# A convolution stage spread over two places, channel statistics moved to ScalarE, and two POOL products merged

## The chip, the cores and the metric

One NeuronCore of one Trainium2 chip runs the kernel. The metric is device time in microseconds, from the first to the last instruction and what lies around it; a lower time is better. Engine names follow the profile: PE is TensorE (matrix products), PEld its weight loads, DVE is VectorE, ACT is ScalarE, POOL is GpSimd and SP is SyncE, which here only starts DMAs.

## The reference

The input `x` is 32 x 96 x 56 x 56 in fp32. Two layers follow each other. The first is a ConvNeXt block; the second passes the image as a sequence of 3136 tokens through two Mamba blocks and ends with a batch normalisation over all images and tokens. Cut to what matters:

```
# layer 0
h = conv7x7_depthwise(x) + conv_b
h = gelu(layernorm_c(h) @ w1 + b1) @ w2 + b2
x = transpose(h) * layer_scale + x
# layer 1
seq = tokens(x)                                     # 32 x 3136 x 96
for i in range(2):
    h = layernorm(seq[i]);  xs, z = split(h @ in_w)
    xc = silu(causal_conv4(xs));  dt, Bm, Cm = split(xc @ xproj_w)
    delta = softplus(dt @ dt_w + dt_b)
    h_t = exp(delta * A) * h_(t-1) + delta * Bm * xc    # 192 channels x 16 states
    y = (sum_s h * Cm + Dp * xc) * silu(z);  seq = seq + y @ out_w
out = fus_w @ concat(seq, relu(mean(x) @ gp_w)) + fus_b
out = (out - mean_bhw(out)) * rsqrt(var_bhw(out) + eps) * bn_g + bn_b + x
```

The last line needs the mean and the variance of `out` per channel over 32 x 3136 values: these are the statistics that the change moves.

## The kernel before, in words

An image is cut in four chunks of 784 tokens (`CH`), a chunk in two halves of 392 (`HC`). A *stage* is one chunk of one image in one of the two Mamba layers, so there are 32 x 4 x 2 = 256 stages. The order alternates: from stage 2 on, even stages are layer `i == 1` and odd stages are layer `i == 0` of the next chunk.

A stage has 24 *steps* (`NSTEP`): six groups `j` of 32 channels times four groups `g` of four states. Step `n` is `scan(n)`: on DVE a product `w` (L847) of the spread `u` in PSUM with the row `B`, then the recurrence (L854, TENSOR_TENSOR_SCAN) that writes one of four slots of the ring `h`; then POOL multiplies the slot with `C` (L858), and three steps later (`LAG`) `add_up` sums it on PE into `y` (L891). ACT computes the factor `exp(delta*A)` (L805) one or two steps ahead. For `j` in `POOLED` (2 and 5, steps 8 to 11 and 20 to 23) the product `w` is made by POOL instead (L831), so there DVE has only scans to do.  `spread` (L820) is a selection product on PE that brings `u` into PSUM for four steps; it is issued at the end of steps 3, 7, 11, 15 and 23, where DVE's product of the following step needs it.

All other work of the kernel is cut into pieces and laid into the steps by hand. A piece is a pair of a slot number and a function; slot 12.4 means "after the scan of step 12, ordered by 0.4 among the pieces there", a negative slot belongs to the stage before, one of 24 and more to the stage after, and a piece marked `True` runs on DVE ahead of the scan of its step. Every engine's queue keeps this order (`manual_schedule`). The pieces are:

- `prep` of the next stage: layer norm of `seq` (centre, square, mean, root at slots 11 to 13, `norm` on DVE within step 15), projections, `softplus` (writes `dl` at step 4), the products `u = dl * xc` on POOL (L655), and the DMAs that lay `u` out for the pooled groups (`uu`, `us`) and `delta` for the exps (`d4`, three buffers).
- `post` of the stage before: `project` (7.5), `move` from PSUM into `seq` on ACT (L750, slots 9 and 10) and, when the stage before was layer 1, `stat` (L757): two bn_stats on DVE (L760) within step 13, a DMA of their 12 numbers per channel into `stats_d`, and the DMA of `seq` into `o_d`. This falls into odd stages.
- `block0`: half a chunk of layer 0 in each of stages 2 to 249: centre, square, mean and root (L371, L372) at slots 11.3 to 12.8, `norm` on DVE (L419, writes `hz`) ahead of scan 14, then `up` (L424), gelu, `down` (L443) and the residual on ACT (L450) at 18.3.
- `conv`: the depthwise convolution for images 11 to 31. The first 11 images are convolved before the stages begin. For the rest there are three groups of seven images, 48 pairs of channels each, so 144 pieces of work, one in each of stages 2 to 145. Two channels of 56 rows lie on 112 partitions; a vertical band matrix (`band`, 112 x 7 x 112) holds the taps, and seven products (L503), one per horizontal tap, sum 7 images x 56 columns = 392 columns in PSUM. `load` brings `band` and `xpad` (one buffer each) at slot -10, the taps run at 7.7 to 10.4, and `store` at 11.05 adds the bias on ACT (L512) and sends the result to `conv_d` (L515).

PSUM tile `ps2`, which the taps write, has one buffer that the layer-0 block, the projections and the taps use in turn. The tag `sq` has three buffers for squares and the convolution's output. `seq` has four.

After the stages, bn_aggr (L967) makes the mean and the variance of the stored statistics, and a last loop reads `o_d` and `x1_d` and writes the output.

Of the kernel before, what the change touches and what calls it, by code (L numbers as in the profile page):

```python
# [34 lines left out]
F32 = mybir.dt.float32  # L35
I32 = mybir.dt.int32
AF = mybir.ActivationFunctionType
ALU = mybir.AluOpType
AX = mybir.AxisListType
# [4 lines left out]
L = H * W  # L44
C = 96
# [6 lines left out]
NCH = 4  # L52
CH = L // NCH
HC = CH // 2
# [7 lines left out]
def convnext_mamba_kernel(  # L62
# [31 lines left out]
    nc = tc.nc  # L94
    B = x.shape[0]

    dram = ctx.enter_context(tc.tile_pool(name="dram", bufs=1, space=DRAM))
# [3 lines left out]
    NB = 7  # L101
    b0 = B - 3 * NB if B > 3 * NB else B
    groups = [(0, b0)] + [(b, b + NB) for b in range(b0, B, NB)]
    conv_d = [
        dram.tile([C * H, (hi - lo) * W], F32, name=f"conv_d{lo}", tag=f"conv_d{lo}")
        for lo, hi in groups
    ]
    band_d = dram.tile([C // 2, 2 * H, 7 * 2 * H], F32, name="band_d")
    stats_d = dram.tile([C, B * NCH, 12], F32, name="stats_d")
    x1_d = [dram.tile([C, L], F32, name=f"x1_d{b}", tag=f"x1_d{b}") for b in range(B)]  # L110
    o_d = [dram.tile([C, L], F32, name=f"o_d{b}", tag=f"o_d{b}") for b in range(B)]

# [82 lines left out]
    for i in range(2):  # L195
# [12 lines left out]
        if i == 1:  # L208

            d["res"] = fw1  # L210
            for q in range(NQ):
                ps = sups.tile([128, 512], F32, name="ps", tag="nps")
# [5 lines left out]
                ps = sups.tile([128, 512], F32, name="ps", tag="nps")  # L218
# [29 lines left out]
    for k in range(2):  # L248
        t = const.tile([C + 1, 3 + CH], F32, name=f"hn{k}", tag=f"hn{k}")
        nc.vector.memset(t[C : C + 1, :], 1.0)  # L250
        hns.append(t)
        t = const.tile([C + 1, HC], F32, name=f"hz{k}", tag=f"hz{k}")
# [4 lines left out]
    R2 = 2 * H  # L257
    GB = (b0 + 1) // 2
    cb = const.tile([R2, C // 2], F32, name="cb")
# [69 lines left out]
    with ExitStack() as main:  # L329
# [13 lines left out]
        def tok(a):  # L343
            return slice(a * HC, (a + 1) * HC)
# [138 lines left out]
        xpad = wp.tile([R2, NB, W + 6], F32, name="xpad", tag="xpad", bufs=1)  # L483
        nc.vector.memset(xpad, 0.0)

        def conv(g, p):
            lo, hi = groups[g]
            v = {}

            def load():  # L490
                v["band"] = wp.tile([R2, 7, R2], F32, name="band", tag="band", bufs=1)
                nc.sync.dma_start(v["band"].rearrange("p k n -> p (k n)"), band_d[p])
                nc.sync.dma_start(
                    xpad[:, :, 3 : 3 + W],
                    x[lo:hi, 2 * p : 2 * p + 2, :].rearrange("b c (h w) -> (c h) b w", w=W),
                )

            def taps_(dws):
                def piece():
                    if dws[0] == 0:  # L500
                        v["ps"] = psum(2)
                    for dw in dws:
                        nc.tensor.matmul(  # L503
                            v["ps"][0:R2, 0 : NB * W], v["band"][:, dw, :],
                            xpad[:, :, dw : dw + W], start=(dw == 0), stop=(dw == 6),
                        )

                return piece

            def store():  # L510
                t = wp.tile([R2, HC], F32, name="sq", tag="sq", bufs=3)
                nc.scalar.activation(  # L512
                    t[:, 0 : NB * W], v["ps"][0:R2, 0 : NB * W], AF.Identity, bias=cb[:, p : p + 1]
                )
                nc.sync.dma_start(conv_d[g][p * R2 : (p + 1) * R2, :], t[:, 0 : NB * W])  # L515

            return [
                (-10, load), (7.7, taps_((0,))), (8.2, taps_((1,))), (8.6, taps_((2,))),
                (9.2, taps_((3,))), (9.6, taps_((4,))), (10.2, taps_((5,))), (10.4, taps_((6,))),
                (11.05, store),  # L520
            ]


# [6 lines left out]
        def prep(S):  # L530
# [117 lines left out]
                    nc.sync.dma_start(ddv[a], dl[rows(a)])  # L648
                S.d4 = []

            def product(q):
                def piece():
                    if q == 0:
                        S.u = wp.tile([128, NQ, HC], F32, name="u", tag="u", bufs=1)
                    nc.gpsimd.tensor_tensor(S.u[:, q], v["dl"][:, q], S.xc[:, q], ALU.mult)  # L655

                return piece

            def store_u(k):
                def piece():  # L660
                    j = POOLED[k]
                    if k == 0:
                        v["uu"] = bcd.tile([len(POOLED), 32, CH], F32, name="uu", tag="uu")
                        S.us = {}
                    for a in range(2):
                        r = 64 * a + 32 * (j % 2)
                        nc.sync.dma_start(v["uu"][k, :, tok(a)], S.u[r : r + 32, j // 2, :])

                return piece
# [34 lines left out]
            elif S is stages[3]:  # L704
# [13 lines left out]
                (t[6] + 0.2, silu("z", None)), (t[7], dbl), (t[8], dbl_out),  # L718
                (max(10.2, t[8] + 1.2), load_bc((0, 1))), (max(13.2, t[8] + 2.2), load_bc((2, 3))),
                (t[9], dt), (t[10], softplus),  # L720
                (max(16.2, t[10] + 1), product(0)), (max(17.2, t[10] + 2), product(1)),
                (max(18.3, t[10] + 3.1), store_u(0)), (25.2, product(2)), (26.3, store_u(1)),
                (max(17, t[10] + 2), load_d4(0)), (max(18, t[10] + 3), load_d4(1)),
                (max(20, t[10] + 3.2), load_u(0)), (23, load_d4(2)),
                (26, load_d4(3)), (32.9, load_u(1)), (30, load_d4(4)), (35, load_d4(5)),
# [2 lines left out]
        def post(S):  # L728


            i, b, c = S.i, S.b, S.c
            v = {}

            def project():
                v["ps"] = [psum(0), psum(1)]
                for a in range(2):
                    nc.tensor.matmul(
                        v["ps"][a][0:C, 0:HC], S.d["res"], S.seq[:, tok(a)],
                        start=True, stop=False,
                    )  # L740
                for q in range(NQ):
                    for a in range(2):
                        nc.tensor.matmul(
                            v["ps"][a][0:C, 0:HC], S.d["ow"][rows(a), q, :], S.z[rows(a), q, :],
                            start=False, stop=(q == NQ - 1),
                        )

            def move(a):
                def piece():
                    nc.scalar.activation(  # L750
                        S.seq[:, tok(a)], v["ps"][a][0:C, 0:HC], AF.Identity,
                        bias=batch_bias[b] if i == 1 else 0.0,
                    )

                return piece

            def stat():  # L757
                st = wp.tile([C, 2, 6], F32, name="stat", tag="stat", bufs=2)
                for a in range(2):
                    nc.vector.bn_stats(st[:, a, :], S.seq[:, tok(a)])  # L760
                nc.sync.dma_start(stats_d[:, b * NCH + c, :], st.rearrange("p a k -> p (a k)"))
                nc.sync.dma_start(o_d[b][:, c * CH : (c + 1) * CH], S.seq)
                del seqs[b, c]

            pieces = [(7.5, project), (9, move(0)), (10, move(1))]
            if i == 1:
                pieces.append((13, True, stat))
            return pieces


# [190 lines left out]


    mv = const.tile([C, 2], F32, name="mv")
    with tc.tile_pool(name="sp", bufs=1) as sp:
        stats = sp.tile([C, B * NCH * 2, 6], F32, name="stats")
        nc.sync.dma_start(stats.rearrange("p (n a) k -> p n (a k)", a=2), stats_d)
        nc.vector.bn_aggr(mv, stats)  # L967
    sc = const.tile([C, 1], F32, name="sc")
    nc.scalar.activation(sc, mv[:, 1:2], AF.Sqrt, bias=eps_c[0:C])
    nc.vector.reciprocal(sc, sc)  # L970
# [74 lines left out]
```

## Time and profile before

| what | value |
| --- | --- |
| median of 3 runs | 17518.44 us (17515.35 to 17520.57) |
| the profiled execution's own time | 17504.21 us |
| its span, first to last instruction | 17502.5 us |
| mean granted PE clock | 0.936 |
| busy: DVE, POOL, PE, ACT | 16171.5, 15632.4, 15285.5, 11224.1 us |
| first scan starts / last scan starts | 641.8 us / 17126.4 us |
| DMA moved | 2346.89 MB, 134 GB/s |

A group of instructions in the profile is a line, an engine, an operation, the tile written and the tiles read, their shapes, how many there are, then the busy time with the mean of one in ns, and the idle time of the engine just ahead of them with what ended most of it. PE's products are pipelined: a fp32 product leaves two records, one per pass, and records overlap, so what a product costs is read from the distance of starts. In a list of waits a row is: engine and line that waited, what ended the wait, total us, times, longest. In the timeline a row is start, duration, engine, line and operation, and in brackets the idle time ahead of it.

### The profile page before, as it was taken

What the parts mean: (1) busy time and instruction counts of PE and PEld (TensorE: products, weight loads), DVE (VectorE), ACT (ScalarE), POOL (GpSimd) and SP (SyncE); (2) the same over time, 40 slices, a digit from 0 to 9 for tenths busy, and PEclk for the clock granted to TensorE, in tenths of its full rate; (3) what the DMA queues carried; (4) which work ended last, traced back from release to release, by engine and by line L of the source; (5) the groups of instructions that cost most, each with busy time, mean ns of one, the idle gap of its engine ahead of it and who ended that gap; (6) DMA issues with size and microseconds to landing.
All of it is one profiled execution on the core that took longest, in us unless ns stands there. A gap on an engine that the chain in (4) does not pass through costs nothing. (4 is left out here: it accounts for less than half of the span.)

```text
span 17502.5 us, 212206 instructions
## 1 busy us (share of the span) xinstructions
PE 15285.5 (87%) x65976; PEld 5191.4 (30%) x65976; DVE 16171.5 (92%) x12592; ACT 11224.1 (64%) x17479; POOL 15632.4 (89%) x8993
## 2 busy tenths in 40 slices
PE   7799999999999999999999988888888888888880
PEld 5233333333333333333333322222222222222220
DVE  7499999999999999999999999999999999999994
ACT  1566666666666666666666666666666666666653
POOL 0499999999999999999999999999999999999991
PEclk9799999999999999999999999999999999999985
DMA  4355555555555555555555555555555555555548
GB/s 102 87 139 138 138 135 136 140 139 139 138 135 138 137 140 138 134 137 137 139 139 134 136 126 128 128 125 125 126 129 127 125 126 126 129 127 124 126 116 273
DMA packets 1403525, 2346.89 MB, mean 134 GB/s; under 512 B 627654, under 2 KB 775154, under 8 KB 1402388
## 3 DMA queue, kind: packets, MB, share of 16 engines
q1 hardware_dynamic: 1395220, 2294.77, 53.1%
q10 hardware_dynamic: 7168, 38.54, 0.6%
q8 instruction: 520, 8.52, 0.2%
q14 instruction: 617, 5.05, 0.1%
HBM read 1929.50 MB, written 402.80 MB: 133 GB/s over the span
## 5 line engine op out<-in xcount | busy, mean ns | idle before, releaser
L858 POOL TENSOR_TENSOR da<-h,bc 128x784 f32<-128x784 f32 x6144 | 11295.8, 1863 | 884.9 <-DVE h L854 721.8
L854 DVE TENSOR_TENSOR_SCAN h<-da,st,w 128x784 f32<-128x784 f32 x3072 | 5662.4, 1843 | 314.3 <-ACT st L865 8.6
L891 PE MATMUL y<-da,ssum 128*32 128x392 f32 x24576 | 5086.0, 533 | 562.9 <-POOL da L858 561.2
L847 DVE TENSOR_TENSOR w<-w,bc 128x784 f32<-128x784 f32 x4096 | 3996.0, 976 | 311.0 <-PE w L820 139.5
L831 POOL TENSOR_TENSOR da<-us,bc 128x784 f32<-128x784 f32 x2048 | 3818.4, 1864 | 2.3 <-DMA us<-uu 2.3
L805 ACT ACTIVATE da<-d,A 128x784 f32<-128x784 f32 x4096 | 3753.9, 941 | 44.8 <-DMA d<-dd 28.6
L805 ACT ACTIVATE w<-d,A 128x784 f32<-128x784 f32 x2048 | 1879.6, 918 | 2659.7 <-DVE h L854 2403.2
L854 DVE TENSOR_TENSOR_SCAN h<-w,st,da 128x784 f32<-128x784 f32 x1536 | 2712.5, 1827 | 5.7 <-ACT st L865 4.6
L891 PEld LDWEIGHTS y<-da,ssum 128*32 128x32 f32 x24576 | 1097.3, 114 | 4106.8 <-issue 2359.5
L576 PE MATMUL ps<-hn,wx 97*64 97x392 f32 x12288 | 2260.4, 502 | 7.4 <-DVE hn L564 7.4
L854 DVE TENSOR_TENSOR_SCAN h<-da,w 128x784 f32<-128x784 f32 x1024 | 1826.4, 1784 | 106.7 <-ACT st L865 4.0
L820 PE MATMUL w<-u,sel 64*128 64x392 f32 x4096 | 1032.9, 583 | 719.0 <-DVE h L854 719.0
L655 POOL TENSOR_TENSOR u<-dl,xc 128x392 f32<-128x392 f32 x768 | 791.6, 1031 | 561.3 <-ACT dl L641 561.3
L576 PEld LDWEIGHTS ps<-hn,wx 97*64 97x64 f32 x12288 | 792.0, 136 | 1420.6 <-issue 1098.9
L885 PE MATMUL y<-xc,D 128*128 128x392 f32 x1536 | 796.8, 605 | 306.9 <-DVE z L872 305.2
L351 ACT ACT_TABLE_LOAD x759 | 973.8, 1283 | 14.7 <-PEq L1032 0.8
L854 DVE TENSOR_TENSOR_SCAN h<-w,da 128x784 f32<-128x784 f32 x512 | 872.2, 1766 | 0.0
L360 ACT ACTIVATE sq<-ps 96x392 f32<-96x392 f32 x768 | 340.6, 490 | 827.2 <-PE ps L355 529.7
L503 PE MATMUL ps<-xpad,band 112*112 112x392 f32 x2016 | 816.1, 520 | 0.0
L633 PE MATMUL ps<-dbl,dtw 6*64 6x392 f32 x3072 | 684.2, 509 | 100.3 <-ACT dbl L611 100.3
L820 PEld LDWEIGHTS w<-u,sel 64*128 64x128 f32 x4096 | 327.2, 196 | 1424.7 <-DVE h L854 1262.4
L865 ACT COPY st<-h 128x2 f32<-128x2 f32 x2304 | 417.5, 181 | 426.3 <-DVE h L854 424.9
(112 smaller groups left out, 14111.0 us busy)
## 6 DMA issues: line engine op xcount, KB each, us to landing
bc<-bd SPq DMA_DIRECT2D x4096, 196.0 KB, 5.2
d<-dd SPq DMA_DIRECT2D x6144, 98.0 KB, 2.6
us<-uu SPq DMA_DIRECT2D x2048, 98.0 KB, 2.2
dd<-dl SPq DMA_DIRECT2D x512, 294.0 KB, 3.8
uu<-u SPq DMA_DIRECT2D x1024, 49.0 KB, 1.6
band<-band_d SPq DMA_DIRECT2D x144, 343.0 KB, 7.4
cv<-conv_d SPq DMA_DIRECT2D x256, 147.0 KB, 2.4
xin<-in_x SPq DMA_DIRECT2D x128, 294.0 KB, 3.0
```

The costliest lines, as they stand in the source:

```text
L351: nc.scalar.preload_act_table_set("natural_log_exp_and_others")
L503: nc.tensor.matmul(v["ps"][0:R2, 0 : NB * W], v["band"][:, dw, :], xpad[:, :, dw : dw + W], start=(dw == 0), stop=(dw == 6),)
L576: nc.tensor.matmul(v["x", q][rows(a), 0:HC], weights[:, k, 64 * q : 64 * q + 64], v["hn"][:, o : o + HC], start=(k == 0), stop=(k == last),)
L655: nc.gpsimd.tensor_tensor(S.u[:, q], v["dl"][:, q], S.xc[:, q], ALU.mult)
L805: nc.scalar.activation(e, S.d4[j], AF.Exp, scale=S.d["A"][:, j, g : g + 1])
L820: nc.tensor.matmul(S.u4[:, 512 * a : 512 * a + HC], sel[rows(a), j % 2, :], S.u[rows(a), j // 2, :], start=True, stop=True,)
L831: nc.gpsimd.tensor_tensor(t, S.us[j], S.bcs[g][:, 0, :], ALU.mult)
L847: nc.vector.tensor_tensor(halves(db), S.u4.rearrange("p (a b) -> p a b", a=2)[:, :, 0:HC], halves(S.bcs[g][:, 0, :]), ALU.mult,)
L854: nc.vector.tensor_tensor_scan(ring[:, g, :], S.e.pop((j, g)), db, 0.0 if c == 0 else d["st"][:, j, g : g + 1], ALU.mult, ALU.add,)
L858: nc.gpsimd.tensor_tensor(da, ring[:, g, :], S.bcs[g][:, 1, :], ALU.mult)
L885: nc.tensor.matmul(S.y[:, 0:HC], S.d["D"][:, q, :], S.xc[:, q, :], start=True, stop=False)
L891: nc.tensor.matmul(S.y[r0 : r0 + 32, 0:HC], ssum, da[:, tok(a)], start=False, stop=(g == NG - 1),)
```

## The change

The convolution of a stage is cut in two parts by images: part 0 has the first four of the seven (224 columns), part 1 the last three (168 columns). Part 0's taps stay at slots 7.7 to 10.4 and its store at 11.05; part 1's taps go to slots 18.5 to 22.2 and its store to 22.9. The loads of `band` and `xpad` move from slot -10 to slot -1. The statistics leave DVE: `move` in layer 1 also accumulates the sum per channel (`accum_out`), and at slots 17.2 and 18.2 ACT squares the deviations from the half's own mean and accumulates them; four numbers per channel go to `stats_d` instead of twelve, and the sums are combined at the end by ten DVE operations in place of bn_aggr. The save of `seq` into `o_d` becomes a piece of its own at 12.9. The first two of the three POOL products `u` become one of 784 columns at slot 16.9.

```diff
-            def taps_(dws):
+            def tap(part, dw):
+                first, last = PARTS[part]
                 def piece():
...
+                    nc.tensor.matmul(
+                        v["ps"][0:R2, 0 : (last - first) * W], v["band"][:, dw, :],
+                        xpad[:, first:last, dw : dw + W], start=(dw == 0), stop=(dw == 6),
+                    )
...
-            def store():
-                t = wp.tile([R2, HC], F32, name="sq", tag="sq", bufs=3)
-                nc.scalar.activation(
-                    t[:, 0 : NB * W], v["ps"][0:R2, 0 : NB * W], AF.Identity, bias=cb[:, p : p + 1]
-                )
-                nc.sync.dma_start(conv_d[g][p * R2 : (p + 1) * R2, :], t[:, 0 : NB * W])
+            def store(part):
+                first, last = PARTS[part]
+                n = (last - first) * W
+                def piece():
+                    t = wp.tile([R2, HC], F32, name="sq", tag="sq", bufs=3)
+                    nc.scalar.activation(
+                        t[:, 0:n], v["ps"][0:R2, 0:n], AF.Identity, bias=cb[:, p : p + 1]
+                    )
+                    nc.sync.dma_start(
+                        conv_d[g][p * R2 : (p + 1) * R2, first * W : last * W], t[:, 0:n]
+                    )
...
+            at = (7.7, 8.2, 8.6, 9.2, 9.6, 10.2, 10.4), (18.5, 18.6, 19.2, 20.2, 21.2, 21.3, 22.2)
             return [
-                (-10, load), (7.7, taps_((0,))), (8.2, taps_((1,))), (8.6, taps_((2,))),
-                (9.2, taps_((3,))), (9.6, taps_((4,))), (10.2, taps_((5,))), (10.4, taps_((6,))),
-                (11.05, store),
+                (-1, load), (11.05, store(0)), (22.9, store(1)),
+                *[(at[part][dw], tap(part, dw)) for part in range(2) for dw in range(7)],
             ]
...
-                    nc.gpsimd.tensor_tensor(S.u[:, q], v["dl"][:, q], S.xc[:, q], ALU.mult)
+                    nc.gpsimd.tensor_tensor(
+                        S.u[:, lo:hi], v["dl"][:, lo:hi], S.xc[:, lo:hi], ALU.mult
+                    )
...
-                (max(16.2, t[10] + 1), product(0)), (max(17.2, t[10] + 2), product(1)),
-                (max(18.3, t[10] + 3.1), store_u(0)), (25.2, product(2)), (26.3, store_u(1)),
+                (max(16.9, t[10] + 1.5), product(0, 2)), (max(18.3, t[10] + 3.1), store_u(0)),
+                (25.2, product(2, 3)), (26.3, store_u(1)),
...
+                    nc.scalar.activation(
+                        S.seq[:, tok(a)], v["ps"][a][0:C, 0:HC], AF.Identity, bias=batch_bias[b],
+                        accum_out=v["st"][:, a : a + 1],
+                    )
...
-            def stat():
-                st = wp.tile([C, 2, 6], F32, name="stat", tag="stat", bufs=2)
-                for a in range(2):
-                    nc.vector.bn_stats(st[:, a, :], S.seq[:, tok(a)])
-                nc.sync.dma_start(stats_d[:, b * NCH + c, :], st.rearrange("p a k -> p (a k)"))
+            def stat(a):
+                def piece():
+                    neg = wp.tile([C, 1], F32, name="neg", tag="neg", bufs=2)
+                    nc.scalar.activation(neg, v["st"][:, a : a + 1], AF.Copy, scale=-1.0 / HC)
+                    t = wp.tile([R2, HC], F32, name="sq", tag="sq", bufs=3)[0:C]
+                    nc.scalar.activation(
+                        t, S.seq[:, tok(a)], AF.Square, bias=neg,
+                        accum_out=v["st"][:, 2 + a : 3 + a],
+                    )
+                    if a == 1:
+                        nc.sync.dma_start(stats_d[:, b * NCH + c, :], v["st"])
...
+            def save():
                 nc.sync.dma_start(o_d[b][:, c * CH : (c + 1) * CH], S.seq)
...
-                pieces.append((13, True, stat))
+                pieces += [(12.9, save), (17.2, stat(0)), (18.2, stat(1))]
...
-        nc.vector.bn_aggr(mv, stats)
+        nc.vector.tensor_reduce(part, st[:, :, 0:2], AX.X, ALU.add)
+        nc.vector.tensor_reduce(mean, part, AX.X, ALU.add)
+        nc.vector.tensor_scalar(mean, mean, 1.0 / (B * L), None, ALU.mult)
+        nc.vector.tensor_scalar(dev, st[:, :, 0:2], 1.0 / HC, mean, ALU.mult, ALU.subtract)
+        nc.vector.tensor_tensor(dev, dev, dev, ALU.mult)
+        nc.vector.tensor_scalar(dev, dev, float(HC), None, ALU.mult)
+        nc.vector.tensor_tensor(dev, dev, st[:, :, 2:4], ALU.add)
+        nc.vector.tensor_reduce(part, dev, AX.X, ALU.add)
+        nc.vector.tensor_reduce(var, part, AX.X, ALU.add)
+        nc.vector.tensor_scalar(var, var, 1.0 / (B * L), None, ALU.mult)
```

## The prediction on record

> **What bounds the kernel now.** I read the page's busy table and costliest groups first, then the waits of VectorE, then single stages in the timeline. The 256 stages run from 642 to 17130 us, so a stage is about 64.3 us; everything that pays must pay there, per stage.
>
> ```profile
> PE 15285.5 (87%) x65976; PEld 5191.4 (30%) x65976; DVE 16171.5 (92%) x12592; ACT 11224.1 (64%) x17479; POOL 15632.4 (89%) x8993
> ...
> L854 DVE TENSOR_TENSOR_SCAN h<-da,st,w 128x784 f32<-128x784 f32 x3072 | 5662.4, 1843 | 314.3 <-ACT st L865 8.6
> ...
> L655 POOL TENSOR_TENSOR u<-dl,xc 128x392 f32<-128x392 f32 x768 | 791.6, 1031 | 561.3 <-ACT dl L641 561.3
> ...
> L503 PE MATMUL ps<-xpad,band 112*112 112x392 f32 x2016 | 816.1, 520 | 0.0
> ```
>
> DVE and POOL are both nearly full. Which of them leads is told by who waits: POOL waits for DVE's scan (L858 <- DVE h, 721.8 us in all), while DVE never waits noticeably for POOL. Measured from the scans' ends, POOL's product of step 12, 14 and 16 starts 0.1 us after its scan (POOL is waiting there, 2.9 to 3.5 us a stage) and lags by at most 2.3 us elsewhere, less than the four scans that the ring `h` allows. So DVE sets the stage, and a microsecond of POOL alone is worth nothing. The waits of DVE, in the stages with a convolution (2 to 145) and then in those without, are:
>
> ```profile
> DVE w L847 <- PE w L820: 127.0, 116, 4.8
> ```
>
> ```profile
> DVE hz L419 <- ACT ps L372: 73.8, 69, 2.3
> DVE w L847 <- PE w L820: 12.5, 6, 4.8
> ```
>
> The reader is to see two different stalls. With a convolution DVE waits for PE's spread of `u` (L820) ahead of step 12; without one it waits for the normalisation of `block0` (L419). Averaged from the starts of the scans, step 11 takes 3.97 us with a convolution and 3.28 without; step 13 takes 3.2 and 4.2 (even stages). Stage 46 shows the first, on DVE and PE:
>
> ```profile
> 3635.99 7.05 DVE L854 TENSOR_TENSOR_SCAN h<-w,st,da 128x784 f32<-128x784 f32 x4
> 3644.83 0.98 DVE L847 TENSOR_TENSOR w<-w,bc 128x784 f32<-128x784 f32 x1 [1.79 <-PE w L820]
> ```
>
> ```profile
> 3641.56 0.85 PE L891 MATMUL y<-da,ssum 128*32 128x392 f32 x4
> 3642.34 1.58 PE L503 MATMUL ps<-xpad,band 112*112 112x392 f32 x4
> 3643.85 0.93 PE L820 MATMUL w<-u,sel 64*128 64x392 f32 x4
> ```
>
> PE has no idle time from step 4 to 13 there; the last taps stand straight ahead of the spread. The cause of the backlog is a half-speed clock around steps 4 to 6:
>
> ```profile
> 3625.40:3634.20 8.80, 8.80 (x31) 2.61 (x30) 8.36 (x7) 5.18 (x8) 8.67 (x6) 0.63 0.44 115
> ```
>
> PE, by contrast, has room in steps 19 to 23 (stage 61):
>
> ```profile
> 4634.69 0.93 PE L885 MATMUL y<-xc,D 128*128 128x392 f32 x2 [1.18 <-DVE z L872]
> 4635.54 2.17 PE L891 MATMUL y<-da,ssum 128*32 128x392 f32 x12
> 4638.32 0.85 PE L891 MATMUL y<-da,ssum 128*32 128x392 f32 x4 [0.61 <-POOL da L858]
> 4639.93 0.93 PE L820 MATMUL w<-u,sel 64*128 64x392 f32 x4 [0.75 <-DVE h L854]
> ```
>
> [...] without a convolution PE is idle 3.7 us in steps 7 to 11, and the centring products then take 0.86 us a record instead of 0.49 (granted clock 0.61 from 13538 to 13550). [...] Here Square without one is 490 ns (L360), Identity with one 571 (L750). [...]
>
> **The change part by part.**
>
> *Convolution.* A tap is two passes, 0.33 us apart in the timeline, so 0.66 us; seven are 4.6. Steps 7 to 10 keep 4/7 of the columns, so PE gains 3/7 of 4.6 = 2.0 us ahead of the spread. The excess of step 11 over 3.29 us sums to 103 us over 144 stages (the 127.0 above less the usual 0.17 us gap of 116 waits and less a start-up wait of 4.8 agrees). Clipping each stage's excess by 2.0 leaves 11 us: gain 92. What is late next is `hz` at step 13: ScalarE's exponential for it ends 0.5 to 0.9 us before DVE arrives (even stages), 1.2 to 1.7 (odd). It moves with PE, so no new wait in even stages.
> Part 1 costs PE 7 x 2 passes x 168/392 x 0.33 = 2.0 us, plus about 0.1 us start for each of five isolated groups (first record 0.59 against 0.49): 2.5 us. No row shows 168 columns; if its weight load (L503's LDWEIGHTS, 174 ns a pass, hidden now behind 0.33) bounds a pass instead of the 0.14 that I take, it is 14 x 0.174 + 0.5 = 2.9; nothing can make it less than 2.0. The idle time shown above is 1.18 + 0.61 + 0.75 = 2.5. The spread of the next step 0 then starts about when it does now; it ends 0.9 us before DVE needs it (4640.8 against 4641.7), which is the cover. Behind part 1's store on ACT stand the exps of steps 25 on, needed over 3 us later. The store itself is one more ACTIVATE: 83.2 us/144 = 0.58 becomes about 0.44 + 0.39, in ACT idle time.
> On SP, the loads of `band` and `xpad` move from step 14 to 23, behind three d4 loads, cv, x1, uu, us and the new store. They wait for the last tap, at about step 22.5; behind them stand d4(3), needed at step 10, and the second uu store, needed at 9. They land in 7.4 and 8.0 us and have 20 us. Cost nothing; were SP held 15 us longer, d4(3) would reach ACT late.
>
> *Statistics.* bn_stats leaves DVE: step 12 is 3.69 us in odd stages and 2.98 in even ones, 0.71 each. In 72 odd stages with a convolution: 51 us. In the 55 without, DVE would only wait for `hz` instead: odd stages take 64.35 us, even ones 64.28, so 0.07 x 55 = 4. ACT gets, in each odd stage, two accumulator reads of 0.19 (L450's row) at steps 9 and 10, and at 17 and 18 two times 0.2 (a small copy, L865: 181 ns) + 0.58 + 0.19 = 1.9 us. ACT is idle there for 3.47 us, waiting for L443 (stage 61); behind them stand the residual (L450), which waits for PE anyhow, and the exps of step 20. On SP the statistics' store moves from 13 to 18 and waits for ACT ahead of x1 and uu, which wait later still. Uncovered it would be 2.3 us x 128 = 295. The 0.4 at steps 9 and 10 delays the third Square at most; I charge 4 us for odd stages whose `hz` slack goes. At the end bn_aggr (7.08 us) becomes ten small operations, about 3.3, and the last stage's statistics cost 0.9 more: gain 3.
>
> *Product.* One of 784 columns costs 1.86 (L858's row) against 2 x 1.03: POOL saves 0.2 x 256 = 51 us, worth 0 since POOL waits for DVE. The product of step 17 comes 0.8 us later, used three steps later.
>
> *Sum:* 92 + 51 + 4 + 3 - 4 = 146 us. From the profiled 17504.2 (span 17502.5) that is 17358; the median of the runs shown is 14.2 higher, so 17372.
>
> **Rivals.** (A) *Only the statistics pay*: after a half-clock spell PE stays late, or `hz` takes over the stall. Then 51 + 4 + 3 = 58: 17460. For it: `hz` is 0.5 us from being late. Against: it is fed by the same PE queue that gets earlier.
> (B) *PE goes cold* in steps 8 to 11, since they are thinned out, and conv stages become as those without: even 63.96 to 64.28, odd 64.61 to 64.28, which cancels; 7 remain: 17511. Against: steps 20 to 22 are idle 2.5 us of 5.2 now and keep the clock; 8 to 10 would be about a quarter idle.
> (C) *Slower: a half clock in steps 18 to 23*, now filled to the brim. A spell of 6.8 us [...] loses 3.4 us of PE work; less the cover of 0.9 it holds the next stage's first DVE product by 2.5. In two thirds of the stages (as often as at steps 4 to 6): 96 x 2.5 = 240, less 146: 17612. It decides from 1.9 us lost in every stage. Against: no half clock shows there today, with less work.
> (D) That the change does not do what it says: the order of instructions has bn_stats gone, and seven taps of 224 and seven of 168 columns at the places named.
>
> **How the numbers follow.** Forecast 0.78 (own range 100 to 180 us of gain: 17338 to 17418), A 0.10, B 0.08, C 0.04. The range takes in the forecast and A: 17338 to 17465. A measurement tells about 0.2%, 35 us, from no change: faster 0.88, same 0.08, slower 0.04.
>
> **What would show it.** Right: step 11 near 3.3 us in conv stages, the L847 <- L820 wait under 40 us, odd and even conv stages both near 63.3 us, stages without unchanged near 64.3, POOL's idle time down by about 1 us a stage with nothing lost. Wrong: new DVE waits for ACT at steps 17 to 19 or for the spread at step 23, or clock below 1 in steps 8 to 11.

## The result, and the profile after

| what | before | after |
| --- | --- | --- |
| median of 5 runs each, us | 17518.44 (17514.75 to 17522.98) | 17438.04 (17421.82 to 17446.45) |
| the profiled execution: own time, span, us | 17504.21, 17502.5 | 17446.45, 17444.6 |
| mean granted PE clock | 0.936 | 0.929 |

The change makes the kernel 80 us faster: ratio 0.9953, 95% interval 0.9938 to 0.9967. 146 us were forecast. The median lies above the forecast's own range (17338 to 17418) and inside the wider one, up to 17465, that takes in rival A. The runs of after spread over 25 us and the profiled one is the slowest of them, so the profiled pair differs by less, 57.9 us of span; the ledger below adds up to that.

The page after has the same groups under new line numbers: the scan is L885 (was L854), DVE's product L878 (L847), POOL's product L889 (L858), the spread L851 (L820), the sum into `y` L922 (L891), `z` L903 (L872), the taps L506 (L503), POOL's `u` L666 (L655). First the busy table and the groups:

```profile
PE 15502.9 (89%) x67992; PEld 5472.5 (31%) x67992; DVE 16064.8 (92%) x12345; ACT 11460.0 (66%) x18647; POOL 15605.6 (89%) x8737
...
L666 POOL TENSOR_TENSOR u<-dl,xc 128x784 f32<-128x784 f32 (+1 forms) x512 | 737.5, 1440 | 564.1 <-ACT dl L652 564.1
L506 PE MATMUL ps<-xpad,band 112*112 112x224 f32 (+1 forms) x4032 | 1003.0, 358 | 0.0
```

The parts of the edit that concern DVE and POOL did to those engines what they say: DVE has 106.7 us less to do, POOL's `u` costs 54 us less (POOL's busy time as a whole 27), and PE is busy for 217 us more. Now the waits of DVE in the stages with a convolution (a row is who waited for what, total us, times, longest), then those in the stages without:

```profile
DVE w L878 <- PE w L851: 122.0, 158, 4.8
DVE z L903 <- PE y L922: 21.8, 19, 1.2
```

```profile
DVE hz L419 <- ACT ps L372: 95.5, 73, 2.3
```

The row that the change should have emptied, DVE's product waiting for the spread, was 127.0 us with 116 waits and is 122.0 with 158. The row alone would say that nothing was gained. It mixes two places, though: the same line waits ahead of step 12 and ahead of step 0. Only the steps, taken apart by the starts of the scans, tell them apart. Sums are over the 144 stages with a convolution:

| where | before | after | difference, us | forecast |
| --- | --- | --- | --- | --- |
| step 11, excess over 3.29 us | 102.6 | 28.3 | -74 | -92 |
| step 12, odd stages | 3.69 each | 2.97 each | -51 | -51 |
| step 19, excess over 2.21 | 3.1 | 23.2 | +20 | 0 |
| step 23, excess over 3.02 | -0.5 | 64.6 | +65 | 0 |
| stages without a convolution: even, odd | 64.21, 64.35 each | 64.21, 64.07 each | -15 | -4 + 4 |
| from the last scan's start to the end | 376.1 | 371.2 | -5 | -3 |

The sum is -60; no other step of these 144 stages changes by more than 1.5 us in sum. A stage with a convolution now takes 64.13 us (even; 63.96 before) or 63.88 (odd; 64.61 before); 63.3 was forecast for both. So the stall ahead of step 12 did shrink, but a new one stands ahead of step 0. In stage 60 the trace shows it on PE and on DVE (start, duration, and in brackets the idle time ahead):

```profile
4553.97 0.54 PE L506 MATMUL ps<-xpad,band 112*112 112x168 f32 x2
4554.45 0.85 PE L922 MATMUL y<-da,ssum 128*32 128x392 f32 x4
4555.23 0.83 PE L506 MATMUL ps<-xpad,band 112*112 112x168 f32 x4
4555.99 0.85 PE L922 MATMUL y<-da,ssum 128*32 128x392 f32 x4
4556.77 0.54 PE L506 MATMUL ps<-xpad,band 112*112 112x168 f32 x2
4557.24 0.93 PE L851 MATMUL w<-u,sel 64*128 64x392 f32 x4
```

```profile
4558.22 0.98 DVE L878 TENSOR_TENSOR w<-w,bc 128x784 f32<-128x784 f32 x1 [1.18 <-PE w L851]
```

No row on PE has an idle time any more, where stage 61 before had 1.18, 0.61 and 0.75: PE works without a pause up to the spread, and DVE stands for 1.18 us.

In about a quarter of the stages there is, on top of that, a *spell*: a stretch in which PE is granted half its clock (0.50 in the trace's records of it). Stage 61 after, step 14 and the steps behind it, on PE and as a window (length, busy time of PE, PEld, DVE, ACT, POOL, the granted clock, DMA share, GB/s):

```profile
4598.72 0.93 PE L851 MATMUL w<-u,sel 64*128 64x392 f32 x4 [1.80 <-DVE h L885]
4599.58 0.90 PE L922 MATMUL y<-da,ssum 128*32 128x392 f32 x4
4600.41 4.29 PE L424 MATMUL ps<-hz,w_sb 97*128 97x392 f32 x6
```

```profile
4600.00:4610.00 10.00, 10.00 (x34) 3.40 (x30) 9.43 (x9) 7.61 (x13) 8.90 (x6) 0.66 0.52 116
```

PE waits 1.80 us for a scan, and the six passes of `up` (L424) just behind then take 4.29 us: the granted clock was 0.50 from 4600.26 to 4607.09, and 1.00 in the 12 us before 4600.

Of the 142 stages from 4 to 145, 36 have such a spell in steps 14 to 18 and 106 have none. Without one, the spread of step 0 starts 2.83 us after scan 22 and step 23 takes 3.21 us; with one, it starts at 3.91 and step 23 takes 4.26 and step 19 2.88. Before, 39 stages had a spell there too, and in them the spread started at 1.87 us, just as in the other stages, and step 23 took 3.02. The spells are not new; what is new is that they cost something.

### The profile page after: what moved, and what is told of

It is laid out like the page before. It is cut to its first block, busy times and chain, and to the rows that moved or that the text cites. A ratio compares the mean times of both kernels' runs of the same rounds, so it can differ in the third digit from the quotient of the medians.

```text
span 17444.6 us, 217495 instructions
## 1 busy us (share of the span) xinstructions
PE 15502.9 (89%) x67992; PEld 5472.5 (31%) x67992; DVE 16064.8 (92%) x12345; ACT 11460.0 (66%) x18647; POOL 15605.6 (89%) x8737
## 5 line engine op out<-in xcount | busy, mean ns | idle before, releaser
L889 POOL TENSOR_TENSOR da<-h,bc 128x784 f32<-128x784 f32 x6144 | 11267.2, 1856 | 855.6 <-DVE h L885 734.9
L885 DVE TENSOR_TENSOR_SCAN h<-da,st,w 128x784 f32<-128x784 f32 x3072 | 5664.5, 1844 | 326.4 <-ACT st L896 8.6
L922 PE MATMUL y<-da,ssum 128*32 128x392 f32 x24576 | 5147.1, 542 | 407.2 <-POOL da L889 403.2
L878 DVE TENSOR_TENSOR w<-w,bc 128x784 f32<-128x784 f32 x4096 | 3996.2, 976 | 300.9 <-PE w L851 132.7
L885 DVE TENSOR_TENSOR_SCAN h<-w,st,da 128x784 f32<-128x784 f32 x1536 | 2712.2, 1827 | 5.9 <-ACT w L836 4.8
L922 PEld LDWEIGHTS y<-da,ssum 128*32 128x32 f32 x24576 | 1094.8, 115 | 3681.1 <-issue 2141.1
L885 DVE TENSOR_TENSOR_SCAN h<-da,w 128x784 f32<-128x784 f32 x1024 | 1827.0, 1784 | 109.1 <-ACT st L896 4.3
L851 PE MATMUL w<-u,sel 64*128 64x392 f32 x4096 | 1026.5, 580 | 655.0 <-DVE h L885 654.0
L666 POOL TENSOR_TENSOR u<-dl,xc 128x784 f32<-128x784 f32 (+1 forms) x512 | 737.5, 1440 | 564.1 <-ACT dl L652 564.1
L506 PE MATMUL ps<-xpad,band 112*112 112x224 f32 (+1 forms) x4032 | 1003.0, 358 | 0.0
L885 DVE TENSOR_TENSOR_SCAN h<-w,da 128x784 f32<-128x784 f32 x512 | 872.3, 1766 | 0.0
L506 PEld LDWEIGHTS ps<-xpad,band 112*112 112x112 f32 x4032 | 583.7, 175 | 832.5 <-issue 770.0
L851 PEld LDWEIGHTS w<-u,sel 64*128 64x128 f32 x4096 | 327.9, 196 | 1255.6 <-DVE h L885 1096.3
```

Source lines behind the costliest of these rows:

```text
L506: nc.tensor.matmul(v["ps"][0:R2, 0 : (last - first) * W], v["band"][:, dw, :], xpad[:, first:last, dw : dw + W], start=(dw == 0), stop=(dw ...
L666: nc.gpsimd.tensor_tensor(S.u[:, lo:hi], v["dl"][:, lo:hi], S.xc[:, lo:hi], ALU.mult)
L851: nc.tensor.matmul(S.u4[:, 512 * a : 512 * a + HC], sel[rows(a), j % 2, :], S.u[rows(a), j // 2, :], start=True, stop=True,)
L878: nc.vector.tensor_tensor(halves(db), S.u4.rearrange("p (a b) -> p a b", a=2)[:, :, 0:HC], halves(S.bcs[g][:, 0, :]), ALU.mult,)
L885: nc.vector.tensor_tensor_scan(ring[:, g, :], S.e.pop((j, g)), db, 0.0 if c == 0 else d["st"][:, j, g : g + 1], ALU.mult, ALU.add,)
L889: nc.gpsimd.tensor_tensor(da, ring[:, g, :], S.bcs[g][:, 1, :], ALU.mult)
```

## The experiments

The theory: the two parts that were sized at nothing are the loss. Part 1 of the convolution takes more PE time in steps 18 to 23 than the idle time and the cover there, which costs a little in every stage, and it has used up the idle time in which PE made good a half-clock spell of steps 13 to 17, which costs a lot in a quarter of them. The rivals: the statistics on ACT, or the one long POOL product, hold something up; or the loss is the residual at step 11, which lies behind the pooling pieces of every eighth stage. Times are medians of 4 to 13 runs, and each ratio is taken against runs of before on the same chip. Those runs of before have medians of 17516 to 17521 us on all chips, so kernels of different chips are set side by side below. Excesses and spells are read from one execution of each kernel.

**The statistics alone.** After, with the convolution and the products of before:

```diff
-                (-1, load), (11.05, store(0)), (22.9, store(1)),
+                (-10, load), (7.7, taps_((0,))), ... (10.4, taps_((6,))),
+                (11.05, store),
```

> Only the statistics are changed; the convolution is whole at its old place and the products are two. Theory 1 (the parts add up; the statistics take 0.71 us from step 12 of every odd stage with a convolution and a little of those without): 51 + 15 + 5 = about 70 us less, 17448. Step 11 keeps its mean of about 4.0 us, step 23 its 3.02, DVE's wait for the spread its 127 us. Rival (the two parts need each other, since the time that DVE saves at step 12 is only waited for elsewhere unless PE is relieved too): under 30 us less, 17490 or more, with new waits of hz on ScalarE in the stages with a convolution.

Measured: 17444.1 us, ratio 0.9957 (0.9945 to 0.9970), 77 us below before. Step 12 in odd stages goes from 3.69 to 2.97; steps 19 and 23 have no excess (-0.6 and 1.0 us). Step 11 keeps its whole stall: 118.9 us of excess, and the row of the spread stays full:

```profile
DVE w L865 <- PE w L838: 139.7, 109, 4.0
```

So ACT's part of the change holds nothing up, and the statistics alone are worth nearly all that the whole change is worth.

**The convolution alone.** Before, with only the divided convolution:

```diff
-                (-10, load), (7.7, taps_((0,))), ... (10.4, taps_((6,))),
-                (11.05, store),
+                (-1, load), (11.05, store(0)), (22.9, store(1)),
```

> Only the convolution is cut in two. Theory 1 (the gain at step 11 is given back at steps 19 and 23, where part 1 uses up PE's idle time): about -74 at step 11, +20 at step 19 and +65 at step 23, which is +11: 17530, within 20 us of before. Rival (what is lost at step 23 comes from ScalarE's statistics at steps 17 and 18 or from the merged product, not from part 1): step 23 stays at 3.02 and the time falls by 70 or more, to 17450 or less.

Measured: 17496.6 us, ratio 0.9988 (0.9980 to 0.9996), 24 us below before. It is lower than I expected, since step 11's excess fell to 8.1 us where I had carried over after's 28. The sign of the loss is as the theory has it: step 23 has 73.0 us of excess and step 19 10.0, with bn_stats still on DVE. The row has more waits than that of before, and is shorter in sum:

```profile
DVE w L858 <- PE w L831: 108.8, 165, 4.8
```

94 us come in at step 11 and 80 go out at steps 19 and 23. The stall is paid again twelve steps later.

**The product alone.** Before, with only the merged POOL product:

```diff
-                    nc.gpsimd.tensor_tensor(S.u[:, q], v["dl"][:, q], S.xc[:, q], ALU.mult)
+                    nc.gpsimd.tensor_tensor(
+                        S.u[:, lo:hi], v["dl"][:, lo:hi], S.xc[:, lo:hi], ALU.mult
+                    )
```

> Only the two first POOL products are merged. Theory 1 (POOL waits for DVE, so its work is worth nothing): POOL busy 50 us less, time within 10 us of before, 17508 to 17528. Rival (POOL sets part of the stage): 30 to 50 us less, 17470 to 17490.

Measured: 17509.75 us, ratio 0.9995 (0.9987 to 1.0003). POOL's busy time falls from 15632.4 to 15599.4 us, and the time is not distinguishable from before: POOL waits for DVE, so what it saves it waits.

**Part 1 packed.** After, with its seven taps in two groups that end before step 21, instead of five that reach to step 22:

```diff
-            at = (7.7, 8.2, 8.6, 9.2, 9.6, 10.2, 10.4), (18.5, 18.6, 19.2, 20.2, 21.2, 21.3, 22.2)
+            at = (7.7, 8.2, 8.6, 9.2, 9.6, 10.2, 10.4), (18.5, 18.6, 18.7, 18.8, 20.2, 20.3, 20.4)
```

> The whole change, with part 1's taps as two groups of four and three at 18.5 to 18.8 and 20.2 to 20.4 instead of five groups at 18.5 to 22.2. Theory 1 (part 1's place decides: with it the spread ahead of step 0 starts 2.83 us after scan 22 in undisturbed stages, 0.95 later than before; fewer groups and no tap behind step 20's POOL results bring it back by 0.5 us or more): step 23 falls from 3.47 to about 3.2 us, 30 to 45 us less than the change, 17395 to 17410. Rival (the half-clock spell of steps 14 to 18 alone holds the spread; the order of the taps is indifferent): step 23 stays at 3.4 or more and the time at 17438 within 15.

Measured: 17368.42 us, ratio 0.9916 (0.9903 to 0.9930), 70 us below after, where 30 to 45 were expected. The same products on PE, only in other places, bring the time to what had been forecast for the change. Stage 60 on PE, then the row of waits:

```profile
4524.61 1.40 PE L506 MATMUL ps<-xpad,band 112*112 112x168 f32 x8
4525.85 0.92 PE L916 MATMUL y<-xc,D 128*128 128x392 f32 x2
4526.71 1.51 PE L922 MATMUL y<-da,ssum 128*32 128x392 f32 x8
4528.15 1.11 PE L506 MATMUL ps<-xpad,band 112*112 112x168 f32 x6
4529.19 1.51 PE L922 MATMUL y<-da,ssum 128*32 128x392 f32 x8
4531.09 0.93 PE L851 MATMUL w<-u,sel 64*128 64x392 f32 x4 [0.39 <-DVE h L885]
```

```profile
DVE w L878 <- PE w L851: 35.9, 43, 4.8
```

PE is 0.39 us early for the spread again. Step 23's excess is 14.1 us, step 19's 13.7. In the 111 stages without a spell in steps 14 to 18 the spread starts at 1.86 us again and step 23 loses nothing (0.7 us in all); what is left lies in the 31 stages with one. Step 11's excess fell as well, from 28.3 to 7.6 us, which was not expected and which the edit does not explain. Two things are cheaper: a group of eight passes and one of six take from start to start 1.24 and 1.04 us, 2.3 in all, where the five groups of stage 60 after take 0.67, 0.47, 0.48, 0.76 and 0.47, together 2.85; and everything is issued before step 21, so that the room behind it can still absorb what is late.

**The pooling pieces later.** After, with the two pooling pieces of every eighth stage moved from steps 5 and 6 to steps 14 and 15:

```diff
-            last = [(21.5, total), (29.9, pool), (30.9, fuse)] if k == 2 * NCH - 1 else []
+            last = [(21.5, total), (38.3, pool), (39.2, fuse)] if k == 2 * NCH - 1 else []
```

> The whole change, with the two small products of the batch mean (pool and fuse, once in eight stages) at slots 14.3 and 15.2 instead of 5.9 and 6.9, behind which PE's queue waits twice for ScalarE. Theory (what is left of the stall at step 11 in the change, 27 of 28 us, lies in those stages, numbers 2 modulo 8, because this round trip follows the half-clock spell): step 11 falls to 3.3 us in all stages, about 25 us less than the change, 17413. Rival (the even stages are late for another reason, such as the load of the input): step 11 keeps 28 us in sum, 17438.

Measured: 17432.76 us, ratio 0.9952 (0.9940 to 0.9965). The residual of step 11 was 28.3 us, 27.4 of it in the 18 stages whose number divided by 8 leaves 2; 17 of them have these pieces, and stage 2 has the rest of it, 1.6 us. It falls to 9.6 and 5.2. The whole time moves by 5 us, within the spread of the runs. So the residual isn't the loss: steps 23 and 19 keep 65.7 and 27.0 us. That the pieces make it is not shown, though. With the pieces at their old place it is 8.1 us with the convolution alone, 7.6 in the packed kernel and 10.6 in the next one; this sum changes from one traced kernel to another by more than the move explains (see *The clock*).

**The clock held up at step 14.** After, plus four passes behind step 14 whose result nobody reads, in the gap behind which the spells begin:

```diff
+            def warm():
+                ps = psum(2)
+                for dw in (0, 6):
+                    nc.tensor.matmul(ps[0:R2, 0 : NB * W], v["band"][:, dw, :],
+                                     xpad[:, :, dw : dw + W], start=(dw == 0), stop=(dw == 6))
...
-                (-1, load), (11.05, store(0)), (22.9, store(1)),
+                (-1, load), (14.25, warm), (11.05, store(0)), (22.9, store(1)),
```

> The whole change, with two more products of 392 columns on PE at step 14 of the stages with a convolution, whose result nobody reads. Theory (PE's 1.7 us of idle time at step 14 lets its clock fall to half in a quarter of these stages, and what PE then loses reaches DVE at steps 19 and 23, since part 1 has used up the idle time there): the spells of steps 13 to 17 go, step 19 returns to 2.2 and step 23 to about 3.2, 50 to 65 us less than the change, 17373 to 17390, although PE does 190 us more work. Rival (the spells don't matter, or PE is simply too full): no gain, or some 20 us more, 17440 to 17460.

Measured: 17370.03 us, ratio 0.9916 (0.9902 to 0.9929): more work on PE, and 68 us less than after. No stage has a spell in steps 13 to 17 any more. Of PE at the same place in stage 60 the trace shows the added passes (here under L531), and behind them `up`, its six passes now in 2.24 us:

```profile
4564.94 1.57 PE L531 MATMUL ps<-xpad,band 112*112 112x392 f32 x4
4566.70 0.93 PE L859 MATMUL w<-u,sel 64*128 64x392 f32 x4 [0.19 <-DVE h L893]
4567.56 0.85 PE L930 MATMUL y<-da,ssum 128*32 128x392 f32 x4
4568.34 2.24 PE L424 MATMUL ps<-hz,w_sb 97*128 97x392 f32 x6
```

```profile
DVE w L886 <- PE w L859: 61.4, 143, 4.8
```

143 waits are left, one a stage, of 0.4 us each without the start-up one. This run divides the two causes: with the spells gone, step 19 has no excess (-0.6) and step 23 has 24.0 us. Step 11 fell too, from 28.3 to 10.6. The three steps together are 82 us, and the traced executions differ by 88; by the medians it is 68, since the one traced here is the fastest of its runs and that of after the slowest. The same number comes from after itself: its 106 stages without a spell hold 19.7 us, 0.19 each, and 144 x 0.19 is 27.

**Five images and two.** After, with part 1 smaller, and part 0 larger:

```diff
-        PARTS = (0, (NB + 1) // 2), ((NB + 1) // 2, NB)
+        PARTS = (0, 5), (5, NB)
```

> The whole change, split five to two (280 and 112 columns) instead of four to three. Theory 1 (a pass of part 1 is bound by its columns, 0.144 us for 168): part 1 costs 14 x 0.047 = 0.65 us less, the spread ahead of step 0 is in time in undisturbed stages, step 23 falls to about 3.2, and step 11 gains some of its stall back: 15 to 40 us less than the change, 17400 to 17423. Rival (a pass is bound by its weight load of 0.17 us, so fewer columns save nothing): passes stay 0.14 us apart, step 23 stays at 3.47, step 11 gets 10 to 20 us worse: 17448 to 17460.

Measured: 17376.01 us, ratio 0.9920 (0.9907 to 0.9934). Step 23's excess is 10.0 us, step 19's 5.7. Part 1's passes of 112 columns start 0.098 us apart, though a weight load of the same shape (112 x 112) takes 175 ns in after: here it lay beside the products and didn't bound them. In the 125 stages without a spell step 23 loses nothing (0.8 us in all), as the theory has it. The whole, 62 us, is more than the 15 to 40 expected, because the spells in steps 13 to 17 also became fewer, 12% of the stages instead of 25 (see *The clock*). Step 11 gained nothing (30.2 us).

**Unread taps where there is no convolution.** The packed kernel, plus seven taps of 224 columns, in the slots of part 0, in each stage without a convolution; nobody reads their result:

```diff
+            elif m >= len(convs) + 2:
+                put(m, idle_taps())
```

> The change with part 1's taps packed as before (18.5 to 18.8, 20.2 to 20.4), and with seven products of 224 columns at part 0's slots in the stages that have no convolution (146 on), whose result nobody reads. Theory (in these stages hz is late at step 13 only because PE's clock falls to half after its idle time in steps 7 to 11): step 13 falls from 4.3 and 4.1 to 3.23 us, 95 to 105 us less than packed alone, about 17270. Rival (hz is late because DVE arrives early there, whatever the clock): step 13 stays above 4, no gain: 17368.

Measured: 17265.28 us, ratio 0.9856 (0.9843 to 0.9870), 103 us below the packed kernel. Stages without a convolution go from 64.29 and 64.10 us to 63.29 and 63.27, and step 13 in them from 4.36 (even) and 4.12 (odd) to 3.22: with PE busy in steps 7 to 10, 1 of the 109 stages from 146 to 254 has half clock in steps 8 to 12, so the centring products keep the full clock in nearly all, and `hz` comes in time. After itself shows the same: 99 of these 109 stages have half clock there, and step 13 takes 4.27 us in them, but 3.20 in the 10 others. The row of `hz` has gone from the first places in these stages; this one now leads:

```profile
DVE z L923 <- PE y L942: 11.4, 8, 3.4
```

**All of them.** The packed taps, the pooling pieces later, the passes at step 14 and the unread taps together; of the edits shown above, these lines:

```diff
+            at = (7.7, 8.2, 8.6, 9.2, 9.6, 10.2, 10.4), (18.5, 18.6, 18.7, 18.8, 20.2, 20.3, 20.4)
...
+                (-1, load), (14.25, warm), (11.05, store(0)), (22.9, store(1)),
...
+            last = [(21.5, total), (38.3, pool), (39.2, fuse)] if k == 2 * NCH - 1 else []
...
+                put(m, idle_taps())
```

> The change with all four edits: taps of part 1 packed, two unread products at step 14 of the stages with a convolution, the batch mean's products late, unread taps in the stages without a convolution. Theory: the gains of the single edits add up where they remove different stalls. From packed with idle taps (17265): step 19's and 23's rest goes (13 + 11 us), step 11's rest of 7 us too: 17235 to 17245. Rival (PE is now too full, so what one stall loses another gets): 17260 or more.

Measured: 17233.99 us, ratio 0.9839 (0.9824 to 0.9854), the fastest of all, 282 us below before. Step 11 has 1.4 us of excess, step 19 -0.7, step 23 1.1, and the wait for the spread is nearly empty:

```profile
DVE w L906 <- PE w L879: 15.3, 11, 4.8
```

**The same with five images and two.**

```diff
-        PARTS = (0, (NB + 1) // 2), ((NB + 1) // 2, NB)
+        PARTS = (0, 5), (5, NB)
```

> All four edits, split five to two. Theory: with part 1 packed and the spells at step 14 gone there is no stall at step 23 left for the smaller part 1 to save, and part 0 is 56 columns a tap more in the backlog ahead of step 12: within 10 us of the four-to-three split, or up to 20 slower. Rival (less work in steps 18 to 23 still pays): 10 to 20 us faster.

Measured: 17256.99 us, ratio 0.9851 (0.9834 to 0.9867), 23 us above the kernel with four and three, a little more than the 20 allowed for. Step 11 has 20.0 us of excess again: once the end of the stage has room, the larger part 0 ahead of step 12 is what costs.

## Why the prediction was half right

*The step that failed* is the one on part 1 of the convolution: "The spread of the next step 0 then starts about when it does now; it ends 0.9 us before DVE needs it (4640.8 against 4641.7), which is the cover." Two terms were wrong in it. The prediction had named a wait for the spread at step 23 as a sign that it was wrong, and that wait came.

The smaller is the size. I summed 2.5 us against 2.5 us of idle time. Stage 60 takes 2.85. The passes were right: within a group of 168 columns they start 0.143 us apart, 2.0 us for fourteen. What is left is 0.85, so each of the five groups between other products costs 0.17 us where I had 0.1. In stages without a spell the spread starts 0.96 us later than before (2.83 against 1.87). The cover was read a little too large: in stage 61 before, the spread ends at 4639.93 + 0.93 = 4640.86, not 4640.8, and DVE's product starts at 4641.70; over 142 stages the cover is 0.83 us on average. After, DVE's product starts about 0.05 us behind the end of a spread that it waits for, so 0.78 could be used. 0.96 less 0.78 is what step 23 loses, 0.19 us a stage: 27 us over 144. The cover was real; I had no reserve beyond it.

The larger is what the idle time was for. Before, 39 of 142 stages ran at half clock somewhere in steps 14 to 18, and the spread of step 0 still started at 1.87 us: PE made the lost time good in the gaps of steps 19 to 23. I looked for half clock in steps 18 to 23, found none (3 of the 142 stages have it there), and took the gaps for free. With them filled, 36 such stages lose 1.24 us at step 23 (44.5 in all, 38 above the 0.19 each) and 0.67 at step 19 (24): 62 us of the 88 lost. The clock experiment removes these and leaves 24.

*The convolution at step 11:* the mechanism was right, the size 74 where I had 92. The residual of 28 us was expected to be 11. Three kernels that keep the pooling pieces in place do have 8 to 11, one of them with the divided convolution alone (a gain of 94), so the 92 was not far off, and part of the 28 may belong to the traced execution. Of the 74, steps 19 and 23 take 85 back in the ledger of the profiled pair, and by the medians too the statistics alone (77 us) are worth nearly the whole 80.

*The statistics:* step 12 gave the 51 us forecast. The ACT work was hidden as argued: no wait of DVE for ACT came up at steps 17 to 19. Its groups after, by shape:

```profile
L783 ACT ACTIVATE sq<-seq,neg 96x392 f32<-96x392 f32 x256 | 159.3, 622 | 8.3
L770 ACT ACTIVATION_READ_ACCUMULATOR seq<-ps,fb 96x1 f32 x256 | 48.5, 189 | 0.0
```

0.62 and 0.19 us stand for my 0.58 and 0.19. (Before, Square without a bias per partition took 490 ns and Identity with one 571; the new Square has one.) In the odd stages without a convolution DVE does wait for `hz` instead (step 13 goes from 3.66 to 4.10 us), but gives back only 0.44 of the 0.71: 15 us of gain where I had 4. I had bounded the odd stages by the even ones, which was too strict. (The even stages take 64.21 us over all of 146 to 253, where I had 64.28, and step 11 takes 4.00, not 3.97, over all 144 stages; neither moves a term by more than 4 us.) The 4 us charged for ACT's accumulator reads did not show in that total; they were not measured alone. The end got 5 us shorter, 3 forecast.

*The product:* worth nothing, as forecast, by its own run. That POOL's idle time would fall by about 1 us a stage did not come true; it fell by 31 us in all, 0.12 a stage, since the stages themselves hardly became shorter.

*The moves on SP's queue* cost nothing that the steps show; they were not tried alone.

*The rivals.* A's 17460 is 22 us from the median, but not for A's reason: the relief at step 11 came, and was taken away at step 23. That the median lies in the range which takes in A is therefore luck. B fell: in steps 7 to 12 a half clock shows in 1 of the 144 stages. C had the mechanism that decided, with the place wrong: spells earlier than steps 18 to 23, not caused by the new work, and let through to DVE by it. It "decides from 1.9 us lost in every stage"; what happened is that about 1.1 us more delay (3.91 less 2.83) in a quarter of them met a cover already used up, and took 62 us where C had 240. D fell with the instructions that the page shows.

*The clock.* I had looked for a loss of clock only where more idle time adds up; that a gap like that of step 14 is harmless was an assumption of mine, and the runs don't bear it out. In after, PE stands at step 14 for 1.7 us on average, and behind this gap the spells come, in a quarter of the stages; four passes put into it end them. On the other hand the 2.5 us of idle time in three pieces at steps 20 to 22 before were followed by a spell in only 3 of 142 stages. Nor do the 3.7 us that the prediction read in the stages without a convolution stand in one piece: they are a sum, and none of its pieces is longer than 2.8 us. The gaps at step 14 behind which a spell came were 2.0 to 2.5 us long before and 1.8 to 2.2 after.

The traces say more about when. In after, 84 of the 142 stages have a gap of 1.7 us or more at step 14, and all 36 spells there stand in these; they begin 0.6 to 1.6 us behind the gap's end. Of the 58 stages with a shorter gap none has one. Before, it is 88 stages, with all 39 spells. With the four passes at step 14 no gap of over 0.4 us is left there. A long gap was not enough, though: 48 stages of after have one and no spell. The length of the gaps also fits that the statistics alone have spells in 1% of the stages there, where before has 28%: before, all 39 spells follow the gaps of the odd stages, which bn_stats makes 2.2 us long; without bn_stats most gaps are 1.5 us.

At other places spells come without such a gap. At steps 3 to 6 they come in 68% of the convolution stages before and in 94% after, and PE is far from idle ahead of them: in after it is busy for 88% or more of the 4 us ahead of each of the 134. Most of the work there, 1559 of 2215 passes, is a product with 6 rows:

```profile
L644 PE MATMUL ps<-dbl,dtw 6*64 6x392 f32 x3072 | 685.7, 509 | 99.6 <-ACT dbl L622 99.6
```

No run changes these products alone, so whether they have to do with the spells is not shown.

*What stays open.* Which of the long gaps at step 14 are followed by a spell, and why half clock comes at steps 3 to 6 with PE busy, no run tells. The shares of stages with a spell (at steps 3 to 6, 68 to 94%) and the residual of step 11 differ from one traced kernel to another. The residual goes with how long the half clock ahead of it lasts: in after the 12 stages with pooling pieces that lose 1.6 us or more at step 11 all have 6.8 us of it, which begin 2.6 to 3.2 us ahead of their step 5, and the 5 that lose under 0.5 us have 3.4 us of it, or (one of them) none. How much of the difference between kernels is chance, one trace of each does not tell.

## What to carry to other kernels

Idle time of an engine that does not lead is not free room: it may be the reserve in which that engine makes good its own bad stages, so look at the bad stages (here a quarter) and not only at a typical one before filling it. Work moved into a gap should go in few groups, at the front of the gap, and the urgent product behind it should be found and its slack measured to better than a tenth of a microsecond; 0.83 us of cover, 0.78 of it of use, against 0.96 us of delay was already a loss. And a row of waits that hardly changes (127.0 to 122.0) can hide a gain and a loss at two places: take it apart by step before reading it.

## What the runs showed of the hardware

- The granted PE clock was 1.00 or 0.50 in the traces of before and after. In after (stages 4 to 145) all 36 spells of steps 14 to 18 followed a gap on PE of 1.7 us or more at step 14; 48 stages had such a gap and no spell, and none of the 58 with a shorter gap had one. At steps 3 to 6, 134 of the 142 stages had a spell with PE busy for 88% or more of the 4 us ahead of it.
- Work whose result nobody reads made the kernel faster by keeping PE's clock: four passes of 392 columns at step 14 took 68 us off the kernel after (mean granted clock of the profiled executions 0.929, then 0.940); seven taps a stage in the stages without a convolution took 103 us off the packed kernel (0.936, then 0.952).
- Within a group, a fp32 pass starts 0.33 us after the one before it at 392 columns, 0.143 at 168 and 0.098 at 112; a group that stands between other products costs 0.14 to 0.17 us beyond its passes (stage 60, packed and after). At 112 columns (five images and two) that is below the 175 ns that a weight load of the same shape takes in after.
- An accumulator read on ACT is an instruction of its own and takes 0.187 to 0.190 us; the small ACTIVATE that makes the negative mean takes 0.191.
